# Second-layer biases of the experts: added at the evacuation of a block's product, or by one product per token tile

## The chip, the cores and the metric

One core of one Trainium2 chip runs the whole kernel, in 32-bit floating point. The metric is the device time of one execution in microseconds (us). The kernel before took 852.11 us, the median of 3 runs (851.6 to 853.08).

Engine names in the profile: PE is TensorE (matrix products and transposes, with PEld for its weight loads), DVE is VectorE, ACT is ScalarE, POOL is GpSimd, SP is SyncE, which here only issues DMAs. PSUM is the memory that TensorE writes its products to; SBUF is the working memory.

## The reference

A perceiver layer on 64 sequences of 32 tokens with 256 features (2048 tokens):

```
x = x + cross_attention(layernorm(x), context)   # context: 257 x 128 per sequence, 16 heads of 64
x = x + self_attention(layernorm(x))             # 4 heads, within each sequence of 32, rotary positions
x = x + experts(x)                               # 8 experts, the 2 best of each token
```

The experts, cut to what matters here (m is a token, n an expert, `ew` the weight of the expert for the token, zero except for two of the eight):

```
scores = x @ Wr.T + br;  idx = top_k(scores + biases, 2);  val = softmax(scores)[idx] / sum
a, b   = split(x @ Wl1[n] + bl1[n])
y[n]   = (silu(a) * b) @ Wl2[n] + bl2[n]
out[m] = sum over n of ew[m, n] * y[n, m]
```

The bias `bl2` enters as the sum over n of `ew[m, n] * bl2[n]`. It can be added for a token at once, as a product of its 8 weights with the 8 x 256 table of biases, or for each expert separately before the weight is applied.

## The kernel before

The 2048 tokens are 16 tiles of 128 rows (`t`), each holding 4 sequences of 32 (`b`). The main loop (L931) walks over 64 pairs (t, b). Each step does the cross attention of one sequence: scores (`s`, L369), softmax, transposes of the probabilities (`tp`, L392), the product with the context (`pa`, L402).

SP and TensorE run in program order: `tc.manual_schedule` hands these two queues to the author. VectorE, ScalarE and GpSimd are ordered by a scheduler. The rest of a tile's work is therefore cut by hand into segments (generators with `yield`) that the loop puts between the steps of the cross attention. `rest(t)` (L597) is one such generator for a tile: `cross_output` (L407), a layer norm, `self_attention` (L442), a second norm into `xr`, and `route` (L526). The table `steps` (L875 to L880) says, for each of the four sequences of a tile, which generator goes one segment on at six places: "near" is the `rest` of the tile just finished, "far" that of the tile before it, "ahead" the projection of queries (done for two tiles at once, so in every second tile). A tile's `rest` has 14 segments: 5 as "near" and 9 as "far".

`route(t)` transposes `xr` (`trr`, L252), computes the router's scores, takes the best two, and forms the weights `ew`, which lie in `xr` beside the 256 features. Two short products `pk` (L567, L568) count the tokens that each expert has so far; from them come the two slots of each token, and two indirect DMAs on the POOL queue (L578) scatter the rows of `xr` into the DRAM array `routed`. Its last two segments add the biases: `pw` (L586) transposes the 8 weights of each token, VectorE copies them to SBUF (L588), `pb` (L591) multiplies them with the bias table `b2_sb` (8 x 256), and VectorE adds the product to x (L592). Then x is stored to the output (L594, L595): from the SP queue for tiles 0 to 13, from the POOL queue for tiles 14 and 15.

After that the experts run in blocks of 128 routed rows (class `Blocks`, L663). `gathered` (L677, SP queue) loads 128 rows of `routed`, `weights` (L683, SP queue) loads the weights of the block's expert into a lane (a pair of SBUF buffers: first layer with its biases, 1028 KB, second layer, 512 KB), with a condition that skips the load when the lane holds that expert already. `prepared` (L693) transposes the rows (`pxT`) and forms the row's gate. `first_half` and `second_half` (L714, L731) do the first layer (`pa`, `pb`, L726) and the activation (L740, L745). `combined` (L752) does the second layer (`py`, L757), scales it by the gate on the way out of PSUM (`y`, L762), and adds it to the output with an indirect DMA on the POOL queue (L763).

Six early blocks (L771) are filled from the tokens of the first tiles and run in two lanes, interleaved by hand with the rest of tiles 14 and 15 (the `do(...)` strings, L1009 to L1022, where "near" and "far" are segments of the two tiles, x, a, b and c the four parts of a block). The late blocks (L800, L1027) follow in three lanes; 28 of them are executed for these inputs. The third lane's second buffer (L988) takes the place of a buffer that held attention probabilities. In the same stretch SP loads the rows `u` (L99) that tile 15's `cross_output` needs for its first product `po` (L431).

Of the kernel before, what the change touches and what calls it, by code (L numbers as in the profile page):

```python
# [9 lines left out]
FP = mybir.dt.float32  # L10
U32 = mybir.dt.uint32
AF = mybir.ActivationFunctionType
ALU = mybir.AluOpType
# [3 lines left out]
P = 128  # L17
D = 256
TOK = 2048
NT = TOK // P  # L20
SEQ = 32
NB = 64
KVD = 128
M = 257
MC = 2
ML = MC * P
XH = 16
HD = 64
AH = 4
NE = 8  # L30
# [2 lines left out]
RW = D + NE + 1  # L33
NBK = (2 * TOK) // P + NE - 1
W1LEN = 2 * 2 * HID + 8
W2LEN = 4 * D
EARLY = 6
LATE = NBK - EARLY
LANES = 3
# [11 lines left out]
def block_kernel(  # L51
# [18 lines left out]
    bias_n: bass.AP,  # L70
    wall1: bass.AP,
    wall2: bass.AP,
    b2: bass.AP,
    out: bass.AP,
):
    nc = tc.nc
# [4 lines left out]
    const = ctx.enter_context(tc.tile_pool(name="const", bufs=1))  # L81
# [3 lines left out]
    ident = const.tile([P, P], FP, name="ident")  # L85
# [12 lines left out]
    def load(dst, src):  # L98
        nc.sync.dma_start(out=dst, in_=src)  # L99


    xs = {}
# [7 lines left out]
    def pool(name, bufs):  # L110
        return ctx.enter_context(tc.tile_pool(name=name, bufs=bufs))
# [34 lines left out]
    wr_sb = const.tile([P, 2, NE], FP, name="wr_sb")  # L146
    br_bc = const.tile([P, NE], FP, name="br_bc")
    bn_bc = const.tile([P, NE], FP, name="bn_bc")
    b2_sb = const.tile([NE, D], FP, name="b2_sb")
    load(awqkv_sb, awqkv.rearrange("(c p) k -> p c k", p=P))  # L150
    load(abqkv_bc, abqkv.partition_broadcast(P))
    load(awo_sb, awo.rearrange("(c p) k -> p c k", p=P))
# [1 line left out]
    load(wr_sb, wr_t.rearrange("(c p) k -> p c k", p=P))  # L154
    load(br_bc, br.partition_broadcast(P))
    load(bn_bc, bias_n.partition_broadcast(P))
    load(b2_sb, b2)

    cos = const.tile([P, 1, 16], FP, name="cos")
    sin = const.tile([P, 1, 16], FP, name="sin")  # L160
# [64 lines left out]
    pp = pool("p", 2)  # L225
    ptp = pool("pt", 2)
    wk = pool("wk", 2)
    sm = pool("sm", 4)
    tb = pool("tb", 1)

    def bank(shape, name):
        return ps.tile([P] + shape, FP, tag="a", name=name)
# [15 lines left out]
    def transposed(dst, src, n, name):  # L248

        pt = bank([n, P], f"tr{name}")  # L250
        for k in range(n):
            nc.tensor.transpose(pt[:, k, :], src[:, k * P : (k + 1) * P], ident)  # L252
        nc.scalar.copy(dst, pt)  # L253
# [188 lines left out]
    def self_attention(t, xn):  # L442
# [80 lines left out]
            nc.tensor.matmul(po, oT[:, k, :], awo_sb[:, k, :], start=(k == 0), stop=(k == 1))  # L523
        nc.vector.tensor_tensor(xs[t], po, xb, ALU.add)

    def route(t, xr):  # L526


        nc.gpsimd.tensor_copy(xr[:, RW - 1 : RW], token[:, t : t + 1])
        xT = wk.tile([P, 2, P], FP, tag="xrT", name=f"xrT{t}")  # L530
        transposed(xT, xr, 2, f"r{t}")
        yield
        pr = bank([NE], f"pr{t}")
        for k in range(2):
            nc.tensor.matmul(pr, xT[:, k, :], wr_sb[:, k, :], start=(k == 0), stop=(k == 1))
        sc = sm.tile([P, NE], FP, tag="rsc", name=f"rsc{t}")
        nc.vector.tensor_tensor(sc, pr, br_bc, ALU.add)
        sel = sm.tile([P, NE], FP, tag="rsel", name=f"rsel{t}")
        nc.vector.tensor_tensor(sel, sc, bn_bc, ALU.add)
        top = sm.tile([P, 8], FP, tag="rtop", name=f"rtop{t}")  # L540
        nc.vector.max(top, sel)
        idx = sm.tile([P, 8], U32, tag="ridx", name=f"ridx{t}")
        nc.vector.max_index(idx, top, sel)
        idf = sm.tile([P, 2, 1], FP, tag="ridf", name=f"ridf{t}")
        nc.vector.tensor_copy(idf[:, :, 0], idx[:, 0:2])

        two = sm.tile([P, 2, NE], FP, tag="rtwo", name=f"rtwo{t}")
        nc.vector.tensor_tensor(
            two, expert_id2, idf.to_broadcast([P, 2, NE]), ALU.is_equal
        )  # L550
        both = sm.tile([P, NE], FP, tag="rboth", name=f"rboth{t}")
        nc.vector.tensor_tensor(both, two[:, 0, :], two[:, 1, :], ALU.add)
        nmx = sm.tile([P, 1], FP, tag="rnmx", name=f"rnmx{t}")
        nc.vector.tensor_reduce(nmx, sc, AX.X, ALU.max, negate=True)
        ex = sm.tile([P, NE], FP, tag="rex", name=f"rex{t}")
        nc.scalar.activation(ex, sc, AF.Exp, bias=nmx)
        nc.vector.tensor_tensor(ex, ex, both, ALU.mult)
        tot = sm.tile([P, 1], FP, tag="rtot", name=f"rtot{t}")
        nc.vector.tensor_reduce(tot, ex, AX.X, ALU.add)
        inv = sm.tile([P, 1], FP, tag="rinv", name=f"rinv{t}")  # L560
        nc.vector.reciprocal(inv, tot)
        ew = xr[:, D : D + NE]
        nc.vector.tensor_scalar(ew, ex, inv, None, ALU.mult)
        yield

        pk = bank([NE], f"pk{t}")
        nc.tensor.matmul(pk, before, both, start=True, stop=False)  # L567
        nc.tensor.matmul(pk, ones, seen, start=False, stop=True)  # L568
        at = sm.tile([P, 1, NE], FP, tag="rat", name=f"rat{t}")
        nc.vector.tensor_tensor(at[:, 0, :], pk, region[:, 0, :], ALU.add)  # L570
        nc.vector.tensor_tensor(seen, seen, both, ALU.add)
        nc.vector.tensor_tensor(two, two, at.to_broadcast([P, 2, NE]), ALU.mult)
        slot = sm.tile([P, 2], FP, tag="rslot", name=f"rslot{t}")
        nc.vector.tensor_reduce(slot, two, AX.X, ALU.add)
        slots = sm.tile([P, 2], U32, tag="rslots", name=f"rslots{t}")
        nc.vector.tensor_copy(slots, slot)
        for k in range(2):
            nc.gpsimd.indirect_dma_start(  # L578
                out=routed[:, :],
                out_offset=bass.IndirectOffsetOnAxis(ap=slots[:, k : k + 1], axis=0),  # L580
                in_=xr,
                in_offset=None,
            )
        yield
        pw = bank([P], f"pw{t}")
        nc.tensor.transpose(pw[:NE, :], ew, ident)  # L586
        ewT = sm.tile([NE, P], FP, tag="rewT", bufs=2, name=f"rewT{t}")
        nc.vector.tensor_copy(ewT, pw[:NE, :])  # L588
        yield
        pb = bank([D], f"pb{t}")  # L590
        nc.tensor.matmul(pb, ewT, b2_sb, start=True, stop=True)  # L591
        nc.vector.tensor_tensor(xs[t], pb, xs[t], ALU.add)  # L592

        queue = nc.sync if t < NT - 2 else nc.gpsimd  # L594
        queue.dma_start(out=out[t * P : (t + 1) * P, :], in_=xs[t])  # L595

    def rest(t, cT, lastT, ut):  # L597

# [50 lines left out]
    def lane_of_queries(i):  # L649
        flat = qp.tile([P, 8, XH, SEQ], FP, tag="q", name=f"lane{i}")  # L650
        flat = flat.rearrange("p a h n -> p (a h n)")
        lanes.append((flat[:, :W1LEN], flat[:, W1LEN : W1LEN + W2LEN]))

# [9 lines left out]
    class Blocks:  # L663
# [88 lines left out]
        def combined(self, b):  # L752
            _, w = lanes[self.lane(b)]
            g = self.gs.pop(b)
            py = bank([D], f"py_{self.name}{b}")
            for j in range(4):
                nc.tensor.matmul(  # L757
                    py, g[:, j * P : (j + 1) * P], w[:, j * D : (j + 1) * D],
                    start=(j == 0), stop=(j == 3),
                )  # L760
            y = xp.tile([P, D], FP, tag="y", bufs=4, name=f"y_{self.name}{b}")
            nc.vector.tensor_scalar(y, py, self.gate[:, b : b + 1], None, ALU.mult)  # L762
            nc.gpsimd.indirect_dma_start(  # L763
                out=out[:, :],
                out_offset=bass.IndirectOffsetOnAxis(ap=self.to[:, b : b + 1], axis=0),
                in_=y,
                in_offset=None,
                compute_op=ALU.add,
            )
# [30 lines left out]
    def late_blocks(done):  # L800
# [75 lines left out]
        ("", "far", "ahead", "near", "far", ""),  # L876
        ("near", "far", "", "near", "far", ""),
        ("ahead", "far", "ahead", "near", "far", "ahead"),
        ("near", "far", "ahead", "", "far", "far"),
    )  # L880
    kvs, probs = {0: context0}, {}
    seqs = [(t, b) for t in range(NT) for b in range(4)]
# [3 lines left out]
    with tc.tile_pool(name="rope", bufs=1) as rp:  # L886
# [27 lines left out]
        c4 = rp.tile([P, 16], FP, name="c4")  # L914
# [3 lines left out]
        c2 = rp.tile([P, 16], FP, name="c2")  # L918
# [12 lines left out]
    for n, (t, b) in enumerate(seqs):  # L931
# [3 lines left out]
        if b == 0:  # L935
            cT = wk.tile([P, XH, 4, SEQ], FP, tag="cT", name=f"cT{t}")
# [17 lines left out]
        pr, pts = probs.pop((t, b)), []  # L954
# [30 lines left out]


    lane_of_queries(1)
    lane2 = pp.tile([P, 4, M], FP, tag="pr", name="lane2b").rearrange("p g m -> p (g m)")  # L988
    lanes.append((kvp.tile([P, W1LEN], FP, tag="kv", name="lane2a"), lane2[:, :W2LEN]))
    load(lanes[2][0], wall1[:P, :])  # L990
    load(lanes[2][1], wall2[:P, :])
# [2 lines left out]
    def do(units):  # L994
        for unit in units.split():
            if unit in work:
                next(work[unit], None)
            else:
                b = int(unit[1:])
                {  # L1000
                    "x": blocks.prepared,
                    "a": blocks.first_half,
                    "b": blocks.second_half,
                    "c": blocks.combined,
                }[unit[0]](b)
                if unit[0] == "c" and b + 2 < EARLY:
                    blocks.weights(b + 2, (0, 1))
# [1 line left out]
    do("near far x0")  # L1009
    blocks.gathered(EARLY - 1)  # L1010
    do("near far near a0 far near b0 near far x1 c0 near a1 near far x2 b1 far a2")
    do("near c1 near far x3 b2 far near c2 far near a3 near x4 b3")
    late, total = late_blocks(done)
    do("c3")
    for b in range(3):
        late.gathered(b)
    do("near a4 near b4 x5 c4")
    late.weights(1, (0, 1))
    do("a5 b5")
    late.prepared(0)  # L1020
# [101 lines left out]
```

## Time and profile before

| what | value |
|---|---|
| time, median of 3 runs (lowest to highest) | 852.11 us (851.6 to 853.08) |
| the profiled execution: its time | 853.89 us |
| the profiled execution: its span, first to last instruction | 851.9 us |
| mean granted TensorE clock in it | 0.986 of full speed |
| POOL busy in the span | 147.4 us, 209 instructions |
| data moved by DMA | 62.71 MB |

The profile is that of one execution. A page lists each engine's busy time; a group of instructions is named by its line, engine and operation, with output and inputs by the program's names, and has a mean duration in ns. In a timeline the columns are start (us from the start of the span), duration, engine, line, operation, output<-input, and in square brackets the idle time of the engine just before it and who released it. Matmuls are pipelined and overlap, so the sum of their durations is more than the time that they take from the engine: the distance between two starts is the better measure. A waits view lists, for an instruction and its releaser, total us waited, how often, and the longest.

### The profile page before, as it was taken

The page shows a single profiled execution, that of the slowest core. Times are in us where ns is not written, and L with a number is a line of the kernel's source. Part 1 is how long each engine was busy: PE and PEld are TensorE (multiplying, and loading weights), DVE is VectorE, ACT ScalarE, POOL GpSimd, SP SyncE. Part 2 cuts the span into 40 slices and gives each one's busy share as a digit, 9 for nine tenths or more (in the row PEclk, how much of TensorE's full clock was granted, in tenths as well). Part 3 has the DMA queues.
Part 4 walks back from the last instruction along what each step waited for, and adds up shares of the span by engine and source line. Part 5 has one row for each costly group of instructions (what it writes and reads, how often), then busy time and mean ns, then how long its engine had stood idle before and what let it go on. Part 6 is the DMA issues. An engine that isn't in the chain of part 4 may idle for free. (4 is left out here: it accounts for less than half of the span.)

```text
span 851.9 us, 15173 instructions
## 1 busy us (share of the span) xinstructions
PE 794.0 (93%) x5240; PEld 611.9 (72%) x5240; DVE 489.2 (57%) x2006; ACT 382.3 (45%) x1082; POOL 147.4 (17%) x209
## 2 busy tenths in 40 slices
PE   4899999999999999999999999999949999999994
PEld 3567677677767766776766777666647799999993
DVE  2456656766676676667676666767626733333331
ACT  2565545455455445546554545554414332222220
POOL 5001011111101011121101011110112422322222
PEclk9999999999999999999999999999979999999997
DMA  8421102020120202021120202012061297357321
GB/s 300 125 53 53 63 1 72 1 85 19 55 75 11 74 0 86 7 67 37 49 72 2 72 1 72 20 53 55 1 258 13 69 318 216 47 110 221 52 38 22
DMA packets 32031, 62.71 MB, mean 74 GB/s; under 512 B 5256, under 2 KB 22672, under 8 KB 30416
## 3 DMA queue, kind: packets, MB, share of 16 engines
q1 hardware_dynamic: 25424, 52.65, 19.0%
q0 software_dynamic: 6528, 9.06, 6.0%
q8 instruction: 43, 0.70, 0.3%
q14 instruction: 36, 0.29, 0.1%
HBM read 83.23 MB, written 13.16 MB: 113 GB/s over the span
## 5 line engine op out<-in xcount | busy, mean ns | idle before, releaser
L374 ACT ACTIVATE pr<-s,nmx 128x257 f32<-128x257 f32 x256 | 120.8, 479 | 72.6 <-DVE nmx L373 71.4
L369 PE MATMUL s<-kv,q 128*128 128x257 f32 x512 | 143.4, 389 | 7.6 <-ACT pr L374 7.6
L373 DVE TENSOR_REDUCE nmx<-s 128x1 f32<-128x257 f32 x256 | 103.8, 420 | 61.7 <-PE s L369 59.9
L402 PE MATMUL pa<-pt,kv 128*128 128x512 f32 x256 | 123.3, 604 | 5.0 <-ACT ov L426 5.0
L369 PEld LDWEIGHTS s<-kv,q 128*128 128x128 f32 x512 | 88.8, 192 | 25.1 <-ACT pr L374 12.2
L396 ACT COPY pt<-tp 128x512 f32<-128x512 f32 x128 | 75.9, 593 | 65.2 <-PE tp L392 65.1
L392 PEld LDWEIGHTS tp<-ident,pr 128*128 128x128 f32 x512 | 60.7, 144 | 33.7 <-issue 20.9
L392 PE MATMUL tp<-ident,pr 128*128 128x128 f32 x512 | 81.4, 280 | 1.2 <-DVE pr L381 1.1
L381 DVE TENSOR_SCALAR pr<-pr,inv 128x256 f32<-128x256 f32 x256 | 80.5, 357 | 2.9
L405 ACT COPY cT<-pa 128x512 f32<-128x512 f32 x64 | 37.5, 586 | 88.7 <-PE pa L402 88.7
L578 POOL DMA_INDIRECT routed<-xr,rslots x32 | 32.8, 1025 | 250.7 <-DVE pr L381 105.4
L402 PEld LDWEIGHTS pa<-pt,kv 128*128 128x128 f32 x256 | 44.9, 190 | 40.6 <-issue 29.1
L345 PE MATMUL pqh<-xqT,xwq_sb 128*128 128x256 f32 x256 | 62.5, 389 | 4.3 <-ACT xqT L253 4.3
L763 POOL DMA_INDIRECT out_x<-y_late,to_late x28 | 43.4, 1550 | 110.3 <-DVE gate_late L705 41.4
L435 PE MATMUL po<-xwo_sb,ov 128*128 128x256 f32 x256 | 61.9, 386 | 0.0
L345 PEld LDWEIGHTS pqh<-xqT,xwq_sb 128*128 128x128 f32 x256 | 48.6, 195 | 11.6 <-ACT xqT L253 4.7
L435 PEld LDWEIGHTS po<-xwo_sb,ov 128*128 128x128 f32 x256 | 49.7, 194 | 7.1
L379 DVE RECIPROCAL inv<-sums 128x2 f32<-128x2 f32 x128 | 20.6, 161 | 55.9 <-ACT pr L374 55.2
L745 DVE SCALAR_TENSOR_TENSOR g_late<-pb_late,lane,sa_late 128x128 f32<-128x128 f32 x72 | 20.3, 343 | 55.5 <-PE pb_late L726 37.0
L374 ACT ACTIVATION_READ_ACCUMULATOR pr<-s,nmx 128x1 f32 x256 | 51.8, 203 | 0.0
L410 POOL TENSOR_TENSOR xb<-x,xbo_bc 128x256 f32<-128x256 f32 x16 | 11.6, 725 | 213.7 <-issue 198.5
L450 PE MATMUL pqkv<-awqkv_sb,xaT 128*128 128x512 f32 (+1 forms) x128 | 43.9, 486 | 0.0
(256 smaller groups left out, 1286.5 us busy)
## 6 DMA issues: line engine op xcount, KB each, us to landing
lane<-in_wall SPq DMA_DIRECT2D x24, 1028.0 KB
lane<-in_wall SPq DMA_DIRECT2D x24, 512.0 KB
lane2a<-in_wall SPq DMA_DIRECT2D x10, 1028.0 KB
kv<-in_ctx_t SPq DMA_DIRECT2D x16, 514.0 KB
kv<-in_ctx_a SPq DMA_DIRECT2D x16, 512.0 KB
lane2b<-in_wall SPq DMA_DIRECT2D x10, 512.0 KB
xg_late<-routed SPq DMA_DIRECT2D x28, 132.5 KB
x<-in_x SPq DMA_DIRECT2D x16, 128.0 KB
```

Of the source, the lines that this page charges most:

```text
L345: nc.tensor.matmul(pq[:, mm, :], xwq_sb[:, k, m * P : (m + 1) * P], xqT[:, k, :], start=(k == 0), stop=(k == 1),)
L369: nc.tensor.matmul(s, qb[:, g * P : (g + 1) * P], kvT[:, b, :], start=True, stop=True)
L373: nc.vector.tensor_reduce(nmx, s, AX.X, ALU.max, negate=True)
L374: nc.scalar.activation(pr[:, g, :], s, AF.Exp, bias=nmx, accum_out=sums[:, g : g + 1])
L381: nc.vector.tensor_scalar(pr[:, i, :ML], pr[:, i, :ML], inv[:, i : i + 1], None, ALU.mult)
L392: nc.tensor.transpose(tp[:, g * P : (g + 1) * P], pr[:, g, j * P : (j + 1) * P], ident)
L396: nc.scalar.copy(pt, tp)
L402: nc.tensor.matmul(pa, kvA[:, b, j, :], pts[j], start=(j == 0), stop=(j == MC - 1))
L405: nc.scalar.copy(cT[:, :, b, :], pa.rearrange("p (h n) -> p h n", n=SEQ))
L435: nc.tensor.matmul(po, ov[:, m, :], xwo_sb[:, m, :], start=False, stop=(m == XH // 2 - 1))
L450: nc.tensor.matmul(pq, xaT[:, k, :], awqkv_sb[:, k, lo:hi], start=(k == 0), stop=(k == 1))
L763: nc.gpsimd.indirect_dma_start(out=out[:, :], out_offset=bass.IndirectOffsetOnAxis(ap=self.to[:, b : b + 1], axis=0), in_=y, in_offset=Non ...
```

## The change

The bias row of an expert becomes part of its second-layer weights: the row of 4 x 256 numbers that each of the 128 partitions loads grows to 5 x 256, the last 256 of them being the expert's bias, repeated on all 128 rows by the host. `combined` adds it to the product with one more VectorE operation, in front of the scaling, which then reads SBUF and not PSUM. The two last segments of `route` go, with the bias table and its load. The store of x moves to the end of `self_attention`, right behind the addition of the attention's output. The table `steps` and the `do` strings lose two "far" (and, in the tail, two "near") segments for each tile; with that the segment of `pk` falls behind `pa` of a tile's last sequence, where it was between two score products. The third lane's second buffer, now too wide for its old place, takes a buffer of `cT`.

```diff
-W2LEN = 4 * D
+W2LEN = 5 * D
...
-    load(b2_sb, b2)
...
         nc.vector.tensor_tensor(xs[t], po, xb, ALU.add)

+        queue = nc.sync if t < NT - 2 else nc.gpsimd
+        queue.dma_start(out=out[t * P : (t + 1) * P, :], in_=xs[t])
+
     def route(t, xr):
...
-        yield
-        pw = bank([P], f"pw{t}")
-        nc.tensor.transpose(pw[:NE, :], ew, ident)
-        ewT = sm.tile([NE, P], FP, tag="rewT", bufs=2, name=f"rewT{t}")
-        nc.vector.tensor_copy(ewT, pw[:NE, :])
-        yield
-        pb = bank([D], f"pb{t}")
-        nc.tensor.matmul(pb, ewT, b2_sb, start=True, stop=True)
-        nc.vector.tensor_tensor(xs[t], pb, xs[t], ALU.add)
-
-        queue = nc.sync if t < NT - 2 else nc.gpsimd
-        queue.dma_start(out=out[t * P : (t + 1) * P, :], in_=xs[t])
...
             y = xp.tile([P, D], FP, tag="y", bufs=4, name=f"y_{self.name}{b}")
-            nc.vector.tensor_scalar(y, py, self.gate[:, b : b + 1], None, ALU.mult)
+            nc.vector.tensor_tensor(y, py, w[:, 4 * D :], ALU.add)
+            nc.vector.tensor_scalar(y, y, self.gate[:, b : b + 1], None, ALU.mult)
...
-        ("near", "far", "ahead", "", "far", "far"),
+        ("near", "", "ahead", "", "", "far"),
...
-    lane2 = pp.tile([P, 4, M], FP, tag="pr", name="lane2b").rearrange("p g m -> p (g m)")
+    lane2 = wk.tile([P, XH, 4, SEQ], FP, tag="cT", name="lane2b")
+    lane2 = lane2.rearrange("p h b n -> p (h b n)")
...
-    do("near c1 near far x3 b2 far near c2 far near a3 near x4 b3")
+    do("near c1 near far x3 b2 near c2 near a3 near x4 b3")
...
-    do("near a4 near b4 x5 c4")
+    do("a4 b4 x5 c4")
...
-        "wall2": by_row("Wl2", 4),
-        "b2": a["L0_ffn_bl2"],
+        "wall2": np.concatenate(
+            [by_row("Wl2", 4), np.repeat(a["L0_ffn_bl2"], P, axis=0)], axis=1
+        ),
```

More of the change, by code (lines that the diff above doesn't have):

```diff
@@ L72, in block_kernel @@
     wall2: bass.AP,
-    b2: bass.AP,
     out: bass.AP,
@@ L148, in block_kernel @@
     bn_bc = const.tile([P, NE], FP, name="bn_bc")
-    b2_sb = const.tile([NE, D], FP, name="b2_sb")
     load(awqkv_sb, awqkv.rearrange("(c p) k -> p c k", p=P))
```

## The prediction, made before the changed kernel was run

> **What bounds the kernel now.** I read the page's busy times first, then the waits in front of TensorE, then busy time by stage, then the timelines around every instruction that the change touches.
>
> ```profile
> PE 794.0 (93%) x5240; PEld 611.9 (72%) x5240; DVE 489.2 (57%) x2006; ACT 382.3 (45%) x1082; POOL 147.4 (17%) x209
> ```
>
> TensorE is busy 93% of the span. The windows (columns: length, then busy PE, PEld, DVE, ACT, POOL, clock, DMA share, GB/s) say where the other 7% is:
>
> ```profile
> 200.00:300.00 100.00, 97.91 (x646) 70.63 (x645) 67.61 (x268) 52.28 (x147) 12.45 (x18) 1.00 0.16 50
> ...
> 620.00:640.00 20.00, 11.46 (x94) 9.60 (x95) 4.69 (x21) 3.47 (x8) 3.31 (x4) 0.74 0.66 261
> 700.00:750.00 50.00, 50.00 (x383) 47.70 (x382) 17.01 (x71) 13.81 (x46) 13.99 (x10) 1.00 0.53 132
> ```
>
> The attention loop (to about 617 us) keeps TensorE 98% full, the late expert blocks (from about 690) keep it full; only the seam at 617–690 has holes. So in the loop a TensorE instruction taken away shortens the time one for one, unless a softmax chain then arrives late; in the late blocks VectorE work is free up to its slack; in the seam waits decide. The waits view (total us, times, longest) lists what can arrive late:
>
> ```profile
> PE po L431 <- DMA u<-u_last: 9.7, 1, 9.7
> ```
>
> Its other rows in the loop are small: scores behind the exponentials (L369) 7.6 us in 10 stalls, the context product behind `ov` (L402) 5.0 us in 14.
>
> **What the Trainium skill says.** (1) "VectorE: DVE Perf Modes", section "Mode 2×_2P": a tensor-scalar operation from SBUF can use both read ports for its one tensor; PSUM has one, and tensor_tensor can't. The trace agrees in direction, not by a factor of two: 128×256 takes 357 ns in place in SBUF (L381), 484 ns out of PSUM (L762), and 425 ns as a tensor_tensor of PSUM and SBUF (L592). (2) "TensorE: Matmul & The Clock Gate", "Architectural detail": ACT and DVE are strict FIFO, GPSIMD too. That is my reason to count what queues behind a waiting store on POOL. (3) "DMA: Bandwidth & Descriptors", "Anatomy of one DMA — SWDGE (gpsimd) path": about 2 us of a DMA is fixed, mostly the write's receipt. Here a dependent store starts 4.4 us after the scatter before it (below): longer, so I use the trace. (4) "TensorE: Matmul & The Clock Gate", Part 1: an idle window of about 3.4 us halves the clock. The trace shows 0.74 in the 620–640 window, after the 9.7 us wait.
>
> **The change, part by part.**
>
> *Removed from TensorE: `pw` (L586) and `pb` (L591), 16 tiles.* The rows show 273 ns and 2×426 ns, but products overlap, so I take distances between starts in the loop:
>
> ```profile
> 433.45 0.60 PE L369 MATMUL s<-kv,q 128*128 128x257 f32 x2
> 433.88 0.27 PE L586 MATMUL pw<-ident,xr 128*8 128x128 f32 x1
> 433.99 1.88 PE L402 MATMUL pa<-pt,kv 128*128 128x512 f32 x4
> 435.80 0.69 PE L591 MATMUL pb<-b_sb,rewT 8*128 8x256 f32 x2
> 436.43 0.65 PE L392 MATMUL tp<-ident,pr 128*128 128x128 f32 x4
> ```
>
> `pw` pushes `pa` by 433.99−433.88 = 0.11; `pb` pushes `tp` by 436.43−435.80 = 0.63. So 0.74 per tile; the 14 tiles finished inside the loop look alike: **−10.4 us** (14×0.74), if no data is late instead. Next is `tp`, whose probabilities are ready some 2.7 us after the last score product; without `pw` and `pb` TensorE gets there after about 2.9 (before: 3.6). That leaves 0.1 to 0.4 of slack: no new stall, but narrow.
>
> *Moved: the two `pk` products (L567, L568, about 0.36) from between two score products to after `pa`.* Same cost on TensorE. In every second tile (no queries projected) the third score product stalls 0.76 on the exponentials, and `pk` now partly fills that stall. Moved behind it, between 0.05 and 0.37 in 7 tiles is lost. I take nothing in the sum, because the chain that it waits for also starts earlier, and keep 7×0.37 = 2.6 as an end. The slots' VectorE steps move along; VectorE is 67–71% busy there.
>
> *Removed from VectorE: the copy of `pw` (271 ns) and the x add (425 ns), 16 times.* VectorE has 30% free in the loop: nothing. Removed too is the load of the 8-row bias table at the start: nothing.
>
> *Moved: the store of x to the end of self-attention.* For tiles up to 13 it is on SP. For most of them it waits nowhere that matters. Tile 13's passed between the lane loads and the `u` loads for which `po` stalls:
>
> ```profile
> 618.44 0.87 SPq L689 DMA_DIRECT2D lane<-in_wall  x2
> 619.36 0.43 SPq L595 DMA_DIRECT2D out_x<-x  x1
> 619.83 2.08 SPq L99 DMA_DIRECT2D u<-u_last  x4
> ```
>
> It now precedes the early blocks' gathers, so `u` is issued 0.43 earlier, and 128 KB of store no longer share its queue; the wider second-layer load adds 128 KB there. **−0.4 us.** But the gathers then wait for tile 13's x add, and VectorE does their gate work two steps later; before, VectorE waited 1.8 us for them and TensorE lost about 1. I set this shift at nothing, between −1.0 and +1.0.
>
> *The store of tile 15 goes on POOL's queue, and that adds a wait.* All writes to the output keep their order, so it waits for the second early scatter to land. Before:
>
> ```profile
> 656.63 1.58 POOL L763 DMA_INDIRECT out_x<-y_early,to_early  x1 [8.30 <-DVE y_early L762]
> 659.39 0.57 POOL L242 TENSOR_TENSOR rstdr<-ver,minus_half 128x1 f32<-128x1 f32 x1 [1.19 <-DVE rslots L576]
> ...
> 664.44 1.62 POOL L763 DMA_INDIRECT out_x<-y_early,to_early  x1 [0.30 <-DVE rnmx L554]
> 668.90 0.61 POOL L595 DMA_DIRECT2D out_x<-x  x1 [2.85 <-DVE rounded_late L623]
> ```
>
> Store after scatter: 668.90−664.44 = 4.46 (the other pair 4.40). In the new order the store stands ahead of tile 15's `rstdr` (L242). The scatter comes at about 656.98, the store at 661.4, `rstdr` at 662.3 instead of 659.39, hence xr, its transposes and all of tile 15's routing 2.8 later: TensorE, in program order, stands before `trr` (660.47 before) until about 663.3 with `py`, the next early products and their blocks queued behind. **+2.8**, between 0 (other work absorbs it) and 4. In the seam the tail's `pb` 0.63+0.62, `pw` 0.11 and a little more go: **−1.4.** Tile 14's store stands before its `rstdr` too, but no scatter is then in flight: hidden.
>
> *Added: one VectorE operation per block.* tensor_tensor with PSUM 425 ns (from L592), then tensor_scalar in SBUF 357 ns (from L381) for 484: +0.30 per block, 34 blocks = 10 us of VectorE. In a late block (5.52 us, TensorE full) VectorE works 1.9 of 5.5 us (17.01 of 50): hidden; what would have to break is 3.6 us of cover. PSUM is released 60 ns earlier. Only the end is exposed: y after the last products but one feeds the last two scatters, which wait one for the other (838.43, then 843.16): **+0.35** (0.425+0.05+0.357−0.484).
>
> *The wider second-layer row.* 640 instead of 512 KB for each of the loads that aren't skipped. DMA share is 0.53 in the late blocks, the loads run two to three blocks (11 to 16 us) ahead, and a lane is now held up to 1 us longer by the bias add: hidden with 5 us left. The third lane's new place in SBUF changes no time.
>
> **Sum.** −10.4 −0.4 +2.8 −1.4 +0.35 = −9.05 us. The profiled execution took 853.89 us (span 851.9 plus 2.0 around it): 844.8. It stands 1.78 above the median 852.11, so on the median's footing **843.1 us**.
>
> **Rivals.**
> A (forecast): as summed, 843.1; own range 841.0 to 845.5 with the small ends above.
> B: the gain is partly given back in the loop. The query-less tiles gain only 0.37 of 0.74 (7×0.37 = 2.6 less) because their scores wait for the exponentials anyway, and the shifted gathers cost 1.0: 846.7. For it: the ten stalls at L369; against: the chain starts earlier as well.
> C: tile 15's store costs nothing, because TensorE has early blocks to do in that time: −2.8 more, 840.3. For it: early blocks are interleaved with tile 15 by hand; against: the SP, PE and POOL orders are fixed around `trr`, and `py` stands behind it.
> D, slower: in the late blocks, the lane's second part is freed later (the bias add now reads it after the last product), SP waits for it in order, and the next gather and first-layer load stand behind on SP. If that or the longer y costs 0.45 per block, 28×0.45 = 12.6 goes against 9: 855.7. It decides from 9.05/28 = 0.32 us per late block. For it: SP is in program order; against: 47.70 us of weight loads in 50 and not one PE wait there now, loads two to three blocks ahead.
> E: the products stay hidden in stalls, nothing moves: about 852. Against: starts at 433.88 and 435.80 follow without idle time.
>
> **How the numbers follow.** A 0.52, B 0.17, C 0.18, D 0.08, E 0.05. The range takes C's lower end (its 840.3 less 0.8 for a gain at the gathers), A and B with another 1.3 (tail wait of 4 instead of 2.8): 839.5 to 848.0. It leaves out D, E and the far ends. A measurement of this kernel tells about 0.2% (1.7 us) from no change. A, B and C end below 850.4: faster 0.87; same 0.05; slower 0.08.
>
> **What would show it.** Rows L586 and L591 are gone and the distance from `pa` to the next `tp` falls from 2.44 to about 1.8 (right), or a wait on `pr` grows at L369 or L392 to several us (B). POOL shows tile 15's store some 4.4 us after the second early scatter with `rstdr` right behind it and TensorE idle 2 to 3 us before `trr` (A), or no such idle time (C). VectorE has rows of about 425 and 357 ns for y. The 700–750 window keeps 50.00 of 50; any new wait on lane loads there is D, and would make the prediction wrong on the other side.

## The result, and the profile after

The changed kernel took 843.94 us (median of 4 runs, 843.19 to 844.83) against 851.86 for the kernel before: a ratio of 0.9907 (95% interval 0.9895 to 0.992), 7.9 us less. Measured once more beside the experiments, the same kernel took 840.13 us (839.63 to 842.32) against 851.4: 0.9875 (0.9859 to 0.9891), 11.3 us less. Both lie in the predicted range of 839.5 to 848.0; the second is outside the forecast's own narrower range of 841.0 to 845.5, and outside the 841 to 844 that I had expected of the repeat. Where the two differ is taken up below. The profiled execution took 844.83 us, its span is 843.1.

The busy line and the windows of the page after (the same columns as before):

```profile
PE 780.6 (93%) x5192; PEld 608.4 (72%) x5192; DVE 490.9 (58%) x2008; ACT 382.8 (45%) x1082; POOL 147.4 (17%) x209
```

```profile
200.00:300.00 100.00, 97.71 (x644) 71.82 (x643) 68.19 (x271) 52.30 (x149) 13.43 (x20) 1.00 0.15 48
...
700.00:750.00 50.00, 50.00 (x381) 47.65 (x381) 19.96 (x82) 13.62 (x45) 15.52 (x10) 1.00 0.43 87
```

TensorE lost 13 us of work and is as full as it was, in the loop and in the late blocks. VectorE carries 19.96 instead of 17.01 us in a window of late blocks, and TensorE still does not wait there. The waits view shows the seam's stall, shorter by 0.8:

```profile
PE po L428 <- DMA u<-u_last: 8.9, 1, 8.9
```

The timeline of TensorE around the place where `pw` and `pb` were: `pk` stands between the context product and the next transposes.

```profile
426.71 0.60 PE L366 MATMUL s<-kv,q 128*128 128x257 f32 x2
427.14 1.88 PE L399 MATMUL pa<-pt,kv 128*128 128x512 f32 x4
428.86 0.28 PE L566 MATMUL pk<-rboth,before 128*128 128x8 f32 x2
429.00 0.37 PE L567 MATMUL pk<-seen,ones 128*128 128x8 f32 x2
429.22 0.64 PE L389 MATMUL tp<-ident,pr 128*128 128x128 f32 x4
429.69 1.03 PE L366 MATMUL s<-kv,q 128*128 128x257 f32 x4
```

From `pa` to `tp` it is 429.22−427.14 = 2.08 us, where it was 2.44; of that `pk` is 0.36 (429.22−428.86). Without `pk` it is 1.72, so `pb` had cost 2.44−1.72 = 0.72.

POOL's timeline around tile 15's store, and TensorE's first instruction behind it:

```profile
646.25 1.57 POOL L751 DMA_INDIRECT out_x<-y_early,to_early  x1 [8.59 <-DVE rtot L558]
650.65 0.62 POOL L524 DMA_DIRECT2D out_x<-x  x1 [2.83 <-DMA out_x<-y_early,to_early]
651.29 0.60 POOL L239 TENSOR_TENSOR rstdr<-ver,minus_half 128x1 f32<-128x1 f32 x1
```

```profile
652.39 0.44 PE L249 MATMUL trr<-ident,xr 128*128 128x128 f32 x2 [2.80 <-DVE xr L242]
```

The store comes 650.65−646.25 = 4.40 us after the scatter began, the norm's `rstdr` at once behind the store, and TensorE has stood idle for 2.80 us.

Where the time went, cut at the self-attention transposes (`trqk`) of tiles 0, 12 and 15, the same instruction in each trace. "Repeat" is the profile of the second measurement:

| stretch | before | after | repeat | forecast of the change | after | repeat |
|---|---|---|---|---|---|---|
| start to tile 0 | 98.21 | 97.97 | 96.41 | 0 | −0.24 | −1.80 |
| tile 0 to 12 | 452.57 | 443.57 | 442.38 | −8.9 (12×0.74) | −9.00 | −10.19 |
| tile 12 to 15 | 94.05 | 92.08 | 91.16 | −1.9 (2×0.74+0.4) | −1.97 | −2.89 |
| tile 15 to the end | 207.08 | 209.43 | 208.53 | +1.75 | +2.35 | +1.45 |
| span | 851.9 | 843.1 | 838.5 | −9.05 | −8.8 | −13.4 |

The two traces are of one kernel and differ by 4.6 us; none of that is the change's doing. The clock accounts for about half. The window from 30 to 40 us, in the kernel before, after and in the repeat, with the granted clock third from the end:

```profile
30.00:40.00 10.00, 7.94 (x39) 6.39 (x40) 5.27 (x20) 6.17 (x22) 0.00 (x0) 0.83 0.30 101
30.00:40.00 10.00, 7.90 (x39) 6.24 (x40) 5.54 (x21) 6.43 (x22) 0.00 (x0) 0.83 0.24 90
30.00:40.00 10.00, 8.11 (x45) 5.95 (x46) 5.67 (x22) 6.34 (x23) 0.00 (x0) 1.00 0.19 68
```

Four of the twelve profiles show 0.83 there, and reach tile 0 at 97.05 to 98.21; the eight with 1.00 reach it at 95.33 to 96.42. So the late start, 1.56 here, goes with a stretch of slow clock, whatever the kernel; what brings it on is open. Another 0.77 lies between `po` and the next norm's transposes (`trs`): 10.57 us at a mean clock of 0.79 after, 9.80 at 0.85 in the repeat. The rest is not explained: in four single tiles the 32 small self-attention products (`pss`) take 0.45 to 0.63 from the first to the last instead of 0.19, and a transpose in the seam stalls 1.27 instead of 0.52. What I compare below is therefore the regular stretch from tile 0 to 12, and medians against the kernel before run beside each.

### The profile page after: what moved, and what is told of

Read it like the earlier page. It is cut to its first block, busy times and chain, and to the rows that moved or that the text cites. A ratio compares the mean times of both kernels' runs of the same rounds, so it can differ in the third digit from the quotient of the medians.

```text
span 843.1 us, 15107 instructions
## 1 busy us (share of the span) xinstructions
PE 780.6 (93%) x5192; PEld 608.4 (72%) x5192; DVE 490.9 (58%) x2008; ACT 382.8 (45%) x1082; POOL 147.4 (17%) x209
## 3 DMA queue, kind: packets, MB, share of 16 engines
q0 software_dynamic: 6528, 9.06, 5.9%
## 4 chain that ended last, share of the span: by engine, by line
PE 79%; DVE 7%; ACT 5%; POOL 3%; issue 3%; DMA 2%; SPq 0%; POOLq 0%; ACTq 0%
PE pa L399 12%; PE s L366 11%; PE tp L389 6%; PE pb_late L713 6%; PE pa_late L713 6%; PE py_late L744 6%; PE po L432 5%; PE pqh L342 5%; PE pqkv L447 5%; PE pov L415 4%; PE pq L321 3%; ACT pr L371 3%; PE py_early L744 1%; DVE pr L378 1%; DVE nmx L370 1%
## 5 line engine op out<-in xcount | busy, mean ns | idle before, releaser
L378 DVE TENSOR_SCALAR pr<-pr,inv 128x256 f32<-128x256 f32 x256 | 78.8, 350 | 3.1
L687 ACT COPY bxT_late<-pxT_late 128x256 f32<-128x256 f32 x28 | 10.4, 372 | 70.2 <-PE pxT_late L685 70.2
```

The source lines that it names most:

```text
L378: nc.vector.tensor_scalar(pr[:, i, :ML], pr[:, i, :ML], inv[:, i : i + 1], None, ALU.mult)
```

## The experiments

**Tile 15's store behind the scatters.** Is the 2.80 us stall the store's doing?

```diff
-        queue = nc.sync if t < NT - 2 else nc.gpsimd
-        queue.dma_start(out=out[t * P : (t + 1) * P, :], in_=xs[t])
+        if t < NT - 1:
+            queue = nc.sync if t < NT - 2 else nc.gpsimd
+            queue.dma_start(out=out[t * P : (t + 1) * P, :], in_=xs[t])
...
+        if t == NT - 1:
+            nc.gpsimd.dma_start(out=out[t * P : (t + 1) * P, :], in_=xs[t])
```

> The changed kernel, with one store moved: tile 15's store of x stands on POOL at the end of the route, behind the early block's scatter, and no longer ahead of tile 15's norm. The orders of the other four engines are the same as in the changed kernel. My theory (the store's wait for the scatter is what TensorE waits for, 2.80 us before trr): the idle time before the last trr falls from 2.80 to under 0.3, and the time is 2.3 to 2.8 us below the changed kernel's, about 841.3. Rival (something else in the seam would be late at the same point, such as the router's VectorE chain or the early blocks' activations): the idle time moves to another instruction, and the time stays at 843.4 to 844.

Measured: 838.02 us, ratio 0.984 (0.9827 to 0.9853). The idle time before `trr` is gone (no gap at `trr` over 0.2 us), and no other wait grew: the stretch from tile 15 to the end is 205.91 us, 2.62 less than in the repeat of the changed kernel. The stall was the store's. The median is 5.9 below the first measurement of the changed kernel, lower than I had expected, and 2.1 below the repeat.

**The products alone taken out of the kernel before.**

```diff
-        pw = bank([P], f"pw{t}")
-        nc.tensor.transpose(pw[:NE, :], ew, ident)
-        ewT = sm.tile([NE, P], FP, tag="rewT", bufs=2, name=f"rewT{t}")
-        nc.vector.tensor_copy(ewT, pw[:NE, :])
         yield
-        pb = bank([D], f"pb{t}")
-        nc.tensor.matmul(pb, ewT, b2_sb, start=True, stop=True)
-        nc.vector.tensor_tensor(xs[t], pb, xs[t], ALU.add)
```

> The kernel before, with pw, pb, their copy and the x add taken out and nothing put in their place: the second-layer bias is left out of the result, everything else keeps its order and its queues (the store at the end of the route, pk between two score products). My theory (the gain is the TensorE time of pw and pb, one for one): 14 x 0.74 in the loop and about 1.7 in the seam, 12 us below the kernel before, about 839.8; the distance from one tile to the next falls by 0.74 on average. Rival (the gain comes from moving the store or pk, or products hide in the stalls of the scores): less than 6 us below, over 846.

Measured: 842.32 us, ratio 0.9891 (0.9875 to 0.9908), 9.4 below the kernel before and not 12. From tile 0 to 12 it took 445.66 us, 6.91 less: 0.58 per tile, not 0.74. The timeline of TensorE, with VectorE's last two scalings, shows where the rest stayed:

```profile
427.25 1.88 PE L402 MATMUL pa<-pt,kv 128*128 128x512 f32 x4
428.71 0.84 DVE L381 TENSOR_SCALAR pr<-pr,inv 128x256 f32<-128x256 f32 x2
428.96 1.03 PE L392 MATMUL tp<-ident,pr 128*128 128x128 f32 x4
429.83 0.38 PE L369 MATMUL s<-kv,q 128*128 128x257 f32 x1
```

The four transposes take 429.83−428.96 = 0.87 us, and 429.69−429.22 = 0.47 in the changed kernel. They wait for the scaled probabilities, in pieces too short to be listed as a stall: the two scalings end at 429.29 and 429.55, and the third and fourth transposes start at 429.44 and 429.69, some 0.15 behind each. The four take 0.65 and 0.87 in alternating tiles, so 0.17 and 0.40 are lost. That is a wait for the softmax chain as in the prediction's rival B, though at the transposes and not at the scores.

**`pk` at its old place in the changed kernel.**

```diff
-        ("near", "", "ahead", "", "", "far"),
+        ("near", "far", "ahead", "", "", ""),
```

> The changed kernel with the table of steps naming pk's segment where it was before, between two score products, instead of behind pa. My theory (pk filled part of a stall of 0.76 in the tiles without queries; the move cost 0.05 to 0.37 in each of 7): about 0.9 us below the changed kernel, 843.0, at most 2.6 below. Rival (the move costs nothing, since the exponentials that the scores wait for start earlier as well): within 0.5 of the changed kernel, 843.4 to 844.4.

Measured: 844.8 us, ratio 0.9917 (0.9901 to 0.9932). Both expectations missed: the old place is slower. Tile 0 to 12 takes 445.59 us, 3.21 more than the changed kernel's repeat and the same as with the products alone removed; the four transposes take 0.64 and 0.87 again. So the move of `pk`, which I had put at nothing or a loss, is worth 0.27 us per tile. The loss that I had feared is there, but small: the third score product stalls 0.84 in every second tile of the changed kernel, and 0.76 in the kernel before and with `pk` at its old place.

**`pk` moved alone, in the kernel before.** `pk` and its slots go behind `pb` for tiles 0 to 13:

```diff
-        ("near", "far", "ahead", "", "far", "far"),
+        ("near", "", "ahead", "", "far", "far"),
...
         pb = bank([D], f"pb{t}")
         nc.tensor.matmul(pb, ewT, b2_sb, start=True, stop=True)
         nc.vector.tensor_tensor(xs[t], pb, xs[t], ALU.add)
+        if t < NT - 2:
+            count_and_scatter()
```

> The kernel before, with pw, pb and the stores as they were; only pk and its slots move behind pb for tiles 0 to 13, so that they stand between the context product and the next transposes. Measured so far, from tile 0 to tile 12: products out alone 6.9 us less than before, products out and pk moved 10.2 less. My theory (without pb the transposes of the probabilities come too early and wait about 0.27 per tile; pk behind pa fills that gap, so the move pays only together with the removal): moved alone it gives under 1.5 us from tile 0 to 12, and the time is 850.5 to 851.7. Rival (the move pays for itself, because the slot operations no longer stand in front of the softmax on VectorE): 3.3 us in the loop, 848.

Measured: 853.61 us, ratio 1.0032 (1.0021 to 1.0044): slower, by 2.2 us; tile 0 to 12 takes 453.58, 1.0 more. The rival falls. The gain stayed under my bound, but I had expected a small gain, and the time missed the 850.5 to 851.7. With `pb` in front of them the transposes wait for nothing (0.49 us for four in the kernel before), so there is nothing to cover, and the stall of the third score product grows here too (0.84 instead of 0.76). The move is worth 3.2 us after the removal and costs 1.0 before it: the two parts are not to be costed apart.

**`pk` one place earlier, ahead of `pa`.** Is it the cover on TensorE, or the order on VectorE?

```diff
-        ("near", "", "ahead", "", "", "far"),
+        ("near", "", "ahead", "", "far", ""),
```

> The changed kernel with pk's segment one place earlier, directly ahead of the context product pa instead of behind it, and still behind the last score product. The distance between the last scores and the next transposes is the same on TensorE; but VectorE now does the five slot operations (0.15 to 0.2 us each) before or among the scalings of the probabilities that those transposes read. Theory 1 (cover: pk's 0.36 us between scores and transposes is what hides the late probabilities, wherever it stands there): two tiles take 73.77 us as in the changed kernel, and the time is that of the changed kernel, 840 to 841. Theory 2 (order on VectorE: pk ahead of the chain puts its slot operations in front of the scaling, and this makes the probabilities late): two tiles take 74.2 to 75.0 us, as with pk at its old place (74.32) or worse, and the time is 844 to 848.

Measured: two tiles take 73.87 us, and 73.77 in the changed kernel; the four transposes take 0.44 in every tile:

```profile
423.85 0.60 PE L366 MATMUL s<-kv,q 128*128 128x257 f32 x2
424.28 0.28 PE L566 MATMUL pk<-rboth,before 128*128 128x8 f32 x2
...
424.64 1.96 PE L399 MATMUL pa<-pt,kv 128*128 128x512 f32 x4
426.44 0.60 PE L389 MATMUL tp<-ident,pr 128*128 128x128 f32 x4
426.88 1.03 PE L366 MATMUL s<-kv,q 128*128 128x257 f32 x4
```

VectorE did begin the five slot operations (424.82) ahead of the last two scalings (425.74). In the loop theory 1 stands: what counts is that 0.36 us of other work lies between the last score product and the transposes, not what VectorE does first. The time, 842.76 us (0.9896, 0.9878 to 0.9914), is above the 840 to 841 expected. From tile 12 to 15 it lost 0.8 against the repeat (91.96 to 91.16), again between `po` and `trs` (10.65 us, at a mean clock of 0.77), and the seam's transpose again waited 1.27.

**Six, then twelve more operations on y in each late block.**

```diff
             nc.vector.tensor_tensor(y, py, w[:, 4 * D :], ALU.add)
+            for _ in range(6 if self.name == "late" else 0):
+                nc.vector.tensor_scalar(y, y, 0.0, None, ALU.add)
             nc.vector.tensor_scalar(y, y, self.gate[:, b : b + 1], None, ALU.mult)
```

> The changed kernel with six more VectorE operations in each late block, each adding zero to y in SBUF (0.357 us each, 2.14 us per block). My theory (VectorE has over 3 us of slack in a late block, so the bias add is hidden): the period of a late block stays 5.52 us, and only the end comes later, by about 2.1 us: 846.1. Rival D (the longer way of y out of PSUM holds up the lane, SP or TensorE): the period grows, by 0.3 to 2.1 us, and the time by 8 to 60 us.

Measured: 842.56 us, ratio 0.9896 (0.9878 to 0.9913). The window of late blocks:

```profile
700.00:750.00 50.00, 50.00 (x384) 47.72 (x383) 35.08 (x135) 13.61 (x45) 16.06 (x11) 1.00 0.38 71
```

VectorE does 35.08 of 50 us and TensorE has not lost a hundredth; the period stays 5.52. After the last `py` product began, the span runs on for 15.40 us instead of 13.09 in the repeat: 2.3, of which the six operations, 302 ns each here and not 357, are 1.8. The median is 2.4 above the repeat's; the 846.1 expected had been reckoned from the first measurement.

> The changed kernel with twelve more VectorE operations in each late block. Measured with six: VectorE busy 35.1 of 50 us instead of 19.9, the period of a late block 5.52 us as before. With twelve the sum is 50.3 of 50 us. My theory (VectorE's free time, 3.3 us per late block, is the only cover that the bias add uses up): the period now grows, by 0.05 to 0.5 us, and with 4.3 us at the end the time is 6 to 18 us above the changed kernel's, 846 to 858. Rival (a wait in order on VectorE or the y buffers bind first): the period grows by over 0.5 us.

Measured: 856.74 us, ratio 1.0063 (1.004 to 1.0087), 16.6 above the changed kernel's repeat. The windows, and the first stall:

```profile
700.00:750.00 50.00, 50.00 (x383) 47.70 (x382) 46.67 (x180) 13.65 (x45) 14.42 (x10) 1.00 0.40 89
750.00:800.00 50.00, 47.22 (x354) 44.43 (x353) 46.81 (x180) 12.51 (x41) 13.33 (x9) 1.00 0.55 149
```

```profile
771.47 0.41 PE L685 MATMUL pxT_late<-ident,xg_late 128*128 128x128 f32 x2 [2.68 <-DMA xg_late<-routed]
```

VectorE is busy 46.67 of 50 us and not the 50.3 that I had added up, as these operations too take 301 ns. The first periods still are 5.52. Then the rows of a block come late. SP issued their gather behind the loads of both parts of a lane:

```profile
761.76 1.06 SPq L676 DMA_DIRECT2D lane<-in_wall  x2
763.36 0.33 SPq L667 DMA_DIRECT2D xg_late<-routed  x1
```

The transposes follow 8.1 us later (771.47). In the repeat such gathers are by then issued 9.2 to 9.8 us ahead; here the lead had shrunk to 5.4 at the block before. For the first-layer load waits until VectorE has read the lane's biases for the activation `g` (for the last time from 761.29 to 761.63), and that stood behind the added operations. After the stall the period is 5.52 again, and the last three are 5.69 to 5.78. The time is in the band of my theory, but the way there, a wait in VectorE's order, is the rival's. SP's fixed order passes it on, as in rival D of the prediction, though from the first-layer part of the lane. It sets in somewhere between six and twelve operations, 1.8 and 3.6 us of added VectorE work per block; the bias add brought 0.3.

**One gather less.** The seam's largest stall is in both kernels. The program issues the gather of early block 5 twice; SP's timeline of the changed kernel (repeat) shows what stands behind the first:

```profile
588.56 15.33 SPq L667 DMA_DIRECT2D xg_early<-routed  x6
604.46 0.88 SPq L676 DMA_DIRECT2D lane<-in_wall  x2
605.38 2.15 SPq L98 DMA_DIRECT2D u<-u_last  x4
```

```diff
-            for i in range(EARLY):
+            for i in range(EARLY - 1):
                 blocks.gathered(i)
```

> The changed kernel without the first of two gathers of early block 5: the program issues that gather twice, and the first time SP stands at it for 15 us until the transposes of early block 0 free a buffer, with the lane loads and tile 15's rows u behind it. My theory (po's stall of 8.9 us is that wait on SP, and the half-speed clock follows from the stall): lane loads and u are issued some 10 us earlier, the stall falls below 2 us, the slow clock goes with it, and the time is 8 to 10 us below the changed kernel's, about 834. Rival (u lands late because the lanes' 1.7 MB are ahead of it in the DMA queues, or because the lane's own buffer comes free late): the stall stays above 5 us, and the gain is under 4 us.

Measured: 829.94 us, ratio 0.9748 (0.9736 to 0.9761), 10.2 below the changed kernel's repeat. SP, and TensorE at `po`:

```profile
589.31 4.14 SPq L667 DMA_DIRECT2D xg_early<-routed  x5
594.01 0.88 SPq L676 DMA_DIRECT2D lane<-in_wall  x2
594.93 1.89 SPq L98 DMA_DIRECT2D u<-u_last  x4
```

```profile
604.15 0.70 PE L428 MATMUL po<-u,lastT 128*128 128x256 f32 x2
```

`u` is issued 10.5 us earlier, the stall is gone, and the granted clock between 600 and 620 us is 1.00 where it was 0.75 after and 0.74 in the repeat. All ten profiles with the wait at `po` (8.55 to 9.74 us) show a slow clock in the seam, and neither of the two without it does. So the slow clock followed from the stall, as the Trainium skill has it ("TensorE: Matmul & The Clock Gate", Part 1: after an idle window the clock of TensorE is halved).

**Both together.**

> The changed kernel with tile 15's store behind the scatters, and without the doubled gather. My theory (the two stalls are independent waits on different queues): the gains add up, 5 to 6 below the changed kernel for the store as measured and 8 to 10 for the gather, so 827 to 831 and below both kernels. Rival (with the seam shorter, the late blocks' rows or lane loads are late in its place): 831 to 836, with a new wait on a DMA at pxT_late or pa_late.

Measured: 827.26 us, ratio 0.9719 (0.9707 to 0.9732), 2.68 below the kernel with one gather less alone. The gains add up, and this version is below both kernels. The end of the expected band that used 5 to 6 us for the store came from comparing with the first measurement of the changed kernel; 2.7 is the store's worth.

## Why the prediction was right, and where it was wrong

- **`pw` and `pb`, 0.74 per tile: mis-sized, 0.83.** I measured `pb` from its own start to `tp`. But it started 435.80−433.99 = 1.81 us after `pa`, while `tp` follows `pa` after 1.72: the 0.09 before its start was its cost too. 0.11+0.72 = 0.83; the regular tiles of the changed kernel gain 0.85 (10.19/12).
- **"No new stall, but narrow": true of the whole change, not of the removal.** In the lines that the prediction shows, the transposes begin 436.43−433.45 = 2.98 after the last score product, not 3.6. Less 0.83 that is 2.15 without `pw` and `pb`, earlier than the probabilities (2.7), and the run with the products alone removed has 2.15 (428.96−426.81). So the removal alone left no slack, and 0.17 and 0.40 are lost. `pk`, 0.36 long, makes it good: in the changed kernel the transposes begin after 2.51 (429.22−426.71), just as the last scaling ends, and only the fourth of them needs that one.
- **`pk` at nothing, with a loss as the far end: wrong in sign.** I asked what stall it had filled at its old place, and not what it would fill at its new one: 3.21 us from tile 0 to 12.
- **Rival B** is refuted for the changed kernel: its transposes take 0.47 in every tile. A wait of its kind, at the transposes, shows in the two runs without the cover.
- **The store of tile 13 and the gathers: −0.4 and 0.** The idle time at `po` fell by 0.8 (after) and 0.5 (repeat). Two runs have the same products in the loop, and differ here in the stores, the gathers and the bias add: the kernel with `pk` at its old place took 58.88 us from tile 13 to 15, the one with the products alone removed 60.71. Of these 1.83, 0.96 lie between `po` and `trs` (9.96 and 10.92 us, at mean clocks of 0.84 and 0.75) and go with the clock. The other 0.87 lie before `po`. There the transposes that free SP's buffer come 0.69 sooner after tile 13, `u` is issued 0.49 sooner after them, and `po` starts 0.30 later after the issue. The 0.49 fits the store's term. The 0.69 falls to the gathers' term, which I had put at nothing between −1.0 and +1.0; that the gathers made it was not tried.
- **Tile 15's store, +2.8: right.** 2.80 idle before `trr` in the trace, 2.7 recovered when it was moved. Rival C is refuted.
- **The seam's products, −1.4:** with the products alone removed, the stretch from tile 15 to the end fell by 1.77 (207.08 to 205.31). Here too the term was too small; 0.83 for each of the two tiles gives 1.66.
- **The bias add, +0.35 at the end, hidden elsewhere: right.** The rows of the changed kernel's y are 425 and 357 ns, those it was costed with:

```profile
L750 DVE TENSOR_SCALAR y_late<-y_late,gate_late 128x256 f32<-128x256 f32 x28 | 10.0, 357 | 1.0
L749 DVE TENSOR_TENSOR y_late<-py_late,lane 128x256 f32<-128x256 f32 x18 | 7.6, 425 | 9.6 <-PE py_late L744 9.6
```

  From the start of the last `py` product to the end it is 12.93 before, 13.23 after and 13.09 in the repeat: 0.2 to 0.3 more. The wider weight row costs nothing that the late windows show. Rival D is refuted for this change: even six times the work that was added left the period at 5.52.

The total of the profiled execution (853.89 to 844.83, −9.06; forecast −9.05) was met more closely than the terms deserve, and that is luck. Behind the common late start this execution took 3.0 us more than the repeat (1.18 in tiles 0 to 12, 0.92 to tile 15, 0.90 after), which stood against a loop and a seam that gain more than I had counted. Without them the stretches from tile 0 on give −11.6; the repeated median says −11.3. Why the small products and the seam's transpose were slow in the one profile and not in the other is open.

## What to carry to other kernels

Cost a removed product from the end of its neighbour before to the start of its neighbour after, in a trace where the neighbours also stand side by side. When TensorE is full, the work that you remove was also somebody's cover: look for what becomes ready just behind it, and put independent work of that length there; here the place of two small products made a third of the gain in the loop (3.21 of 10.19). Before moving a store onto a queue, read what stands behind it there and what it must wait for to land.

## What the runs showed of the hardware

- An 8-row product of 256 columns (`pb`, weights 8×128 loaded twice) cost TensorE 0.72 us, one score product, also in two passes, with all 128 rows and 257 columns 0.43 (427.14−426.71): few rows made it no cheaper. Why it cost more was not tried.
- A store that stood on POOL's queue behind an indirect scatter-add, and depended on it, began 4.00 to 4.61 us after the scatter's start in the twelve traces (4.40 to 4.46 in the kernel before, after and in the repeat).
- Waits of 0.1 to 0.3 us inside a group of four transposes appear as no row of the waits views here; only the distance between starts shows them (0.47 against 0.87).
